# Ordering the last channel groups image by image, moving Toeplitz and piece loads, and whitening 1024 adjacent columns at a time

## The chip, the cores and the metric

The kernel runs on one core of a Trainium2 chip. The metric is the device time of one execution in microseconds. An interval or a share in this document is of that time.

## The reference

The input x has 4 images of 64 channels of 256 x 256 float32 pixels. Two layers follow one another.

```python
# layer 0: a two-dimensional convolution, causal in both directions, one filter per channel
hx = implicit_filter(z, Xw1, Xb1, Xw2, Xb2, Xw3, Xb3, Xwo, Xfreq)   # 256 taps for each channel
hy = implicit_filter(z, Yw1, Yb1, Yw2, Yb2, Yw3, Yb3, Ywo, Yfreq)
k  = outer(hx, hy)                      # separable: a 256 x 256 filter per channel
y  = irfft2(rfft2(x, 512) * rfft2(k, 512) / 512)[:256, :256] + x * bias

# layer 1: whitening of the 64 channels
x1   = y as 64 rows of 4 * 65536 pixels
x1_s = x1[:, ::9]
cov  = x1_s @ x1_s.T / n + 0.01 * I
out  = inverse_sqrt(cov, 5 Newton-Schulz steps) @ (x1 - mean(x1_s))
```

The filter is separable, so the convolution of one channel is a product with one triangular Toeplitz matrix from one side and another from the other side. The whitening needs the samples of every pixel of all images before its first output can be computed.

## The kernel before

**Convolution stage.** The 64 channels are eight groups `g` of eight (`CG`). A step is a group and an image, `(g, n)`; `steps` holds the 32 of them in order. The first six groups run through the four images each; the last two groups are ordered image by image (lines 107 and 108), so that image 0 is complete before image 1 and so on. A step has four channel pairs, `c` = 0, 2, 4, 6. A pair goes through two products. `group` (line 394) computes the first product of one pair and the second product of the pair two places earlier together, in matmuls on halves of the array (line 220), copies the first product out on ScalarE (line 409), and adds x times bias to the second on VectorE (line 412), in place in the x tile. `store` (line 420) then writes the pair to the scratch tensor `y_d[n]` in HBM with two DMAs on SP, and puts nine predicated copies per step in a list `todo`, which take every ninth pixel into `samp[n]`; in the last two groups the list gets 18 of half the size. `pack` works that list off after each group, by the planner's costs: a group earns 2.92 us of credit. `covariance(n)` (line 327) multiplies the samples of an image, 116 matmuls, in the second step of the following image.

**What is loaded when.** All loads of this stage are issued by SP, in program order: the two stores of a group, then an x load, then perhaps a block of Toeplitz matrices, then perhaps a piece. A load of two channels of x has 512 KB. There are four x tiles, and `load_x` runs two steps ahead. Each group's Toeplitz matrices come in eight blocks from the filter taps in HBM (`load_toeplitz`, line 188), into one of three tiles; the table `blocks` says after which group of which step each block is issued.

**Whitening and pieces.** After the last step TensorE does the last second products (`half_group`), packs the last samples with matmuls (`pack_by_pe`), computes the last covariance, and then the chain of small products in `whitening`. `spin` and `busy` are matmuls whose result is not used. What follows is `out = W y + shift`, over 32 pieces of 128 x 4096 elements (2048 KB), eight of each image. The two halves of the partitions are the upper and the lower half of an image. Each of four rounds per piece fills two PSUM banks with four matmuls of 64 x 512; ScalarE evicts one bank and VectorE the other, back into the piece's tile, which is then stored.

**Homes.** A piece lives in one of 13 tiles of 16 KB per partition (`homes`, line 347): tiles of the pools for x (`i`), Toeplitz matrices (`t`), samples (`s`) and a pool `e` whose first tile served as scratch. A tile can take its piece when its old content is used up. `early` (line 378) says after which group of which step SP issues the load of the next piece; nine are in that table and the other four come after the last step. Piece 13 and those after it are loaded by SP into the tile of a piece that has been stored (line 647). The store of the first piece, and those of the pieces that have no successor, are issued by SP; the others by GpSimd (line 644).

Of the kernel before, what the change touches and what calls it, by code (L numbers as in the profile page):

```python
# [38 lines left out]
F32 = mybir.dt.float32  # L39
I32 = mybir.dt.int32  # L40
AF = mybir.ActivationFunctionType
ALU = mybir.AluOpType
# [3 lines left out]
NB, C, L = 4, 64, 256  # L46
P, H2 = 128, 2
EMB, ORDER = 33, 64
PIX = L * L
CG = 8  # L50
# [4 lines left out]
EPS = 0.01  # L55
N_ITER = 5
GW = P + L
FP = 4096

TURN = 6.283185  # L60
# [4 lines left out]
def conv_whiten_kernel(ctx: ExitStack, tc: tile.TileContext, a: dict, out: bass.AP):  # L65
    nc = tc.nc
    x = a["x"]

    const = ctx.enter_context(tc.tile_pool(name="const", bufs=1))
    xpool = ctx.enter_context(tc.tile_pool(name="xpool", bufs=4))  # L70
    epool = ctx.enter_context(tc.tile_pool(name="epool", bufs=2))
    spool = ctx.enter_context(tc.tile_pool(name="spool", bufs=NB))
    tpool = ctx.enter_context(tc.tile_pool(name="tpool", bufs=3))
    o1pool = ctx.enter_context(tc.tile_pool(name="o1pool", bufs=4))
# [3 lines left out]
    y_d = [dram.tile([H2 * C, PIX // H2], F32, tag=f"y{n}", name=f"y_d{n}") for n in range(NB)]  # L78
    g_d = dram.tile([P, GW], F32, tag="g", name="g_d")
    g0_d = dram.tile([2 * CG, GW], F32, tag="g0", name="g0_d")  # L80

# [6 lines left out]
    cols = const.tile([P, 4], F32, tag="cols", name="cols")  # L88
# [9 lines left out]
    bias = const.tile([P, C], F32, tag="bias", name="bias")  # L98

    def load_x(t, g, n, c):  # L100
        nc.sync.dma_start(
            out=t[:, c : c + 2],
            in_=x[n, g][:, c : c + 2],
        )


    steps = [(g, n) for g in range(C // CG - 2) for n in range(NB)]
    steps += [(g, n) for n in range(NB) for g in range(C // CG - 2, C // CG)]

    x_tiles = [xpool.tile([P, CG, H2, L], F32, tag="in", name=f"x{u}") for u in range(4)]  # L110
    for c in range(0, CG, 2):
        load_x(x_tiles[0], *steps[0], c)
        if c == 0:
            nc.sync.dma_start(out=decay, in_=a["decay"])
    nc.sync.dma_start(out=mask, in_=a["mask"])
# [5 lines left out]
    for n in range(NB):  # L121
        t = spool.tile([P, FP], F32, tag="samp", name=f"samp{n}")
        samp.append(
# [9 lines left out]
    def load_pick(lo, hi):  # L133
        for s in range(lo, hi):
            nc.scalar.activation(pick[:, s, :], ident, AF.Copy, scale=rows[:, s : s + 1])

    taps = scratch[:, 11:13, :].rearrange("p a w -> p (a w)")[:, 0:GW]
    nc.gpsimd.memset(taps[:, L:GW], 0.0)  # L140

# [13 lines left out]
    for i in range(3):  # L155
        for u in range(2):
# [3 lines left out]
            arg, k, nxt = (scratch[:, 2 + 3 * i + v, half] for v in range(3))  # L160
# [22 lines left out]
    def new_toeplitz(g):  # L183


        return tpool.tile([P, 2, CG, L], F32, tag="toep", name=f"toep_{g}")

    def load_toeplitz(t, g, f, half, lo=0, hi=CG, issue=nc.sync):
        source, row = (g0_d, f * CG + lo) if g == 0 else (g_d, f * C + g * CG + lo)


        skip = 0 if f == half else HP
        issue.dma_start(
            out=t[half * HP : (half + 1) * HP, f, lo:hi, skip:],
            in_=bass.AP(
                tensor=source.tensor,
                offset=source.offset + row * GW + skip,
                ap=[[1, HP], [GW, hi - lo], [1, L - skip]],
            ),
        )  # L200
# [126 lines left out]
    def covariance(n):  # L327
# [15 lines left out]

    pieces = [(n, q) for n in range(NB) for q in range(PIX // H2 // FP)]


    homes = [
        {"t": (tpool, "toep"), "s": (spool, "samp"), "i": (xpool, "in"), "e": (epool, "extra")}[k]
        for k in "eetssiistitis"
    ]  # L350

    def load_y(i):

        n, q = pieces[i]
        pool, tag = homes[i % len(homes)]
        t = pool.tile([P, FP], F32, tag=tag, name=f"yi_{n}_{q}")
        nc.sync.dma_start(out=t, in_=y_d[n][:, q * FP : (q + 1) * FP])  # L357
        return t

    def load_next():  # L360
        loaded[len(loaded)] = load_y(len(loaded))
# [7 lines left out]


    blocks = {}
    for g in range(1, C // CG):
        first = 16 * g - 14 if g < C // CG - 1 else 16 * g - 22
        for part in range(8):
            k = first + (part * 12 // 8 if g < C // CG - 2 else part)
            blocks[k // 4, k % 4 * 2] = (g, part)

    early = {
        (26, 4): 1, (27, 0): 1, (27, 4): 1, (28, 0): 1, (29, 2): 1, (30, 0): 1, (31, 0): 1, (31, 2): 1, (31, 4): 1
    }  # L380
    orders = [list(range(L // HP)), list(reversed(range(L // HP)))]

# [174 lines left out]
    with tc.manual_schedule(  # L557
        engines={engines.PE, engines.SP, engines.DVE, engines.Activation, engines.Pool}
    ):
        toep = {0: new_toeplitz(0)}  # L560

        for f, lo, hi in ((0, 0, 2), (0, 2, 4), (0, 4, 6), (1, 0, 2), (0, 6, 8), (1, 2, 4), (1, 4, 8)):
            for half in range(2):
                load_toeplitz(toep[0], 0, f, half, lo, hi, nc.scalar if half else nc.sync)
        for c in range(0, CG, 2):
            load_x(x_tiles[1], *steps[1], c)
        for i, (g, n) in enumerate(steps):
            xt = x_tiles[i % 4]
            for c in range(0, CG, 2):
                item = (g, n, c, xt, [])  # L570
                if g == C // CG - 1 and n > 0 and c == 2:
                    covariance(n - 1)
                if len(pending) == 2:
                    group(item, pending.pop(0))
                else:
                    half_group(item, 0)
                pending.append(item)
                if i == 0 and c == 6:

                    fold = const.tile([P, C], F32, tag="fold", name="fold")  # L580
                    nc.vector.tensor_tensor(fold, ident[:, 0:C], ident[:, C:P], ALU.add)

                    nc.scalar.activation(bf[:, 0:1], samp[0][:, 0, 0, C : C + 1], AF.Sqrt)
                if i == 1 and c < CG - 2:
                    load_pick(c // 2 * 3, c // 2 * 3 + 3)

                if i + 2 < len(steps):
                    load_x(x_tiles[(i + 2) % 4], *steps[i + 2], c)
                if (i, c) in blocks:
                    tg, part = blocks[i, c]  # L590
                    if part == 0:
                        toep[tg] = new_toeplitz(tg)
                    lo = part % 2 * CG // 2
                    load_toeplitz(toep[tg], tg, part // 4, part // 2 % 2, lo, lo + CG // 2)
                for _ in range(early.get((i, c), 0)):
                    load_next()
        g, n, c, yt, _ = pending[0]
        for item in pending:
            half_group(item, 1)
            pack(1.0)  # L600
            store(item)

        pack()
        i15 = place(2 * C, rows=C).rearrange("p (u c) -> p u c", u=2)
        for u in range(2):
            nc.gpsimd.tensor_scalar(i15[:, u], ident[0:C, 0:C], 1.5, None, ALU.mult)  # L606
        ones = place(P, rows=C)
        nc.gpsimd.memset(ones, 1.0)
        for lo in range(CG // 2, CG, 2):
            pack_by_pe(g, n, yt, slice(lo, lo + 2))  # L610
        spin(4)
        covariance(NB - 1)
        while len(loaded) < len(homes):
            load_next()
        W, shift = whitening(i15, ones)


    halves = [slice(u * C, (u + 1) * C) for u in range(2)]
    for i, (n, q) in enumerate(pieces):
        yt = loaded.pop(i)  # L620

        v = yt.rearrange("p (v f) -> p v f", v=2)
        o = out[n, q].rearrange("p (v f) -> p v f", v=2)

        part = 512 if i == 0 else 1024 if i == 1 or i > len(pieces) - 3 else 2048
        for w in range(FP // 1024):


            cols = slice(w * 512, (w + 1) * 512)
            po = [  # L630
                psA.tile([P, 512], F32, tag="psA", name=f"po_{n}_{q}_{w}_{u}") for u in range(2)
            ]
            for k in range(2):
                for u in range(2):
                    nc.tensor.matmul(  # L635
                        po[u][halves[k]], lhsT=W[halves[u]], rhs=v[halves[u], k, cols],
                        start=True, stop=True,
                    )
            nc.scalar.activation(v[:, 0, cols], po[0], AF.Identity, bias=shift)  # L639
            nc.vector.tensor_scalar(v[:, 1, cols], po[1], shift, None, ALU.add)  # L640
            end = (w + 1) * 512
            if end % part == 0:

                issue = nc.sync if i == 0 or i + len(homes) >= len(pieces) else nc.gpsimd
                issue.dma_start(out=o[:, :, end - part : end], in_=v[:, :, end - part : end])  # L645
        if i + len(homes) < len(pieces):
            loaded[i + len(homes)] = load_y(i + len(homes))

# [57 lines left out]
```

## Time and profile before

| | |
|---|---|
| median of 3 runs | 902.56 us (902.16 to 902.67) |
| span of the profiled execution | 902.1 us |
| own time of the profiled execution | the profile gives none beside the span |
| TensorE matmuls busy | 781.2 us (87%) |
| VectorE busy | 581.5 us (64%) |
| ScalarE busy | 395.5 us (44%) |
| DMA, whole span | 285.61 MB, 317 GB/s |
| HBM read and written | 149.35 MB and 134.44 MB |
| mean granted TensorE clock | 0.927 |

PE is TensorE's matmul, PEld its weight load, DVE is VectorE, ACT is ScalarE, POOL is GpSimd, SP is SyncE; SPq is SP's sequencer, which issues DMAs. In a list of slices each digit is the busy share of a fortieth of the span in tenths; PEclk is the granted TensorE clock in tenths. In the chain and the timelines a row begins with its start and its length in us. In the table of waits a row ends with the total us, the number and the longest of the waits. In a row by stretches of time the engines come first, and the last three numbers are the granted clock, the busy share of the DMA engines and GB/s.

### The profile page before, as it was taken

The page shows a single profiled execution, that of the slowest core. Times are in us where ns is not written, and L with a number is a line of the kernel's source. Part 1 is how long each engine was busy: PE and PEld are TensorE (multiplying, and loading weights), DVE is VectorE, ACT ScalarE, POOL GpSimd, SP SyncE. Part 2 cuts the span into 40 slices and gives each one's busy share as a digit, 9 for nine tenths or more (in the row PEclk, how much of TensorE's full clock was granted, in tenths as well). Part 3 has the DMA queues.
Part 4 walks back from the last instruction along what each step waited for, and adds up shares of the span by engine and source line. Part 5 has one row for each costly group of instructions (what it writes and reads, how often), then busy time and mean ns, then how long its engine had stood idle before and what let it go on. Part 6 is the DMA issues. An engine that isn't in the chain of part 4 may idle for free.

```text
span 902.1 us, 28046 instructions
## 1 busy us (share of the span) xinstructions
PE 781.2 (87%) x11928; PEld 647.5 (72%) x11928; DVE 581.5 (64%) x801; ACT 395.5 (44%) x676; POOL 14.5 (2%) x40
## 2 busy tenths in 40 slices
PE   8999999999999999999999999999999565666200
PEld 7999999999999999999999999999533111212000
DVE  3487778877888778877888877877688332233200
ACT  2655554545455555545454444442487232233200
POOL 1000000000000000000000000000010000000000
PEclk9999999999999999999999999999999766866755
DMA  7988889798788888888997899979999999999998
GB/s 209 327 262 252 242 261 271 234 273 251 247 263 261 244 264 259 258 250 267 293 275 241 285 351 356 335 237 390 375 401 429 430 432 432 429 434 430 430 430 355
DMA packets 117912, 285.61 MB, mean 317 GB/s; under 512 B 8891, under 2 KB 91116, under 8 KB 110108
## 3 DMA queue, kind: packets, MB, share of 16 engines
q1 hardware_dynamic: 113436, 244.94, 79.0%
q0 software_dynamic: 3056, 37.95, 10.0%
q8 instruction: 95, 1.56, 0.7%
q10 hardware_dynamic: 1296, 0.93, 0.4%
q14 instruction: 29, 0.24, 0.1%
HBM read 149.35 MB, written 134.44 MB: 315 GB/s over the span
## 4 chain that ended last, share of the span: by engine, by line
PE 74%; DMA 11%; another core or an unknown queue 7%; DVE 0%; issue 0%; SPq 0%; ACT 0%; POOLq 0%; DVEq 0%
PE p L220 64%; DMA out_dram<-yi 5%; DMA yi<-y_d 5%; PE po L635 4%; PE pc L333 2%; PE ph L252 1%; PE pk L300 1%; PE spin L442 1%; DMA toep<-g_d 0%; PE busy L152 0%; PE pm L158 0%; SPq L357 0%; DMA scratch<-in_zw_dram 0%; DVE yi L640 0%
## 5 line engine op out<-in xcount | busy, mean ns | idle before, releaser
L220 PE MATMUL p<-toep,x 64*64 64x64 f32 (+3 forms) x5040 | 579.5, 284 | 0.8 <-issue 0.8
L220 PE MATMUL p<-toep,o 64*64 64x64 f32 (+3 forms) x5040 | 579.5, 284 | 0.0
L220 PEld LDWEIGHTS p<-toep,x 64*128 64x128 f32 (+1 forms) x5040 | 535.7, 166 | 24.4 <-issue 1.3
L220 PEld LDWEIGHTS p<-toep,o 64*128 64x128 f32 (+1 forms) x5040 | 536.7, 166 | 10.7 <-issue 0.2
L409 ACT COPY o<-p 64x512 f32<-64x512 f32 x504 | 292.8, 581 | 294.2 <-PE p L220 286.6
L319 DVE COPY_PREDICATED samp<-mask,x 128x464 f32<-128x464 int32 (+3 forms) x351 | 297.2, 847 | 9.8 <-DVE x L412 0.2
L412 DVE SCALAR_TENSOR_TENSOR x<-x,bias,p 128x512 f32<-128x512 f32 x252 | 179.8, 744 | 121.3 <-PE p L220 117.3
L635 PE MATMUL po<-yi,chain 64*64 64x512 f32 x1024 | 143.7, 720 | 60.4 <-DMA yi<-y_d 60.4
L640 DVE TENSOR_SCALAR yi<-po,shift 128x512 f32<-128x512 f32 x128 | 96.1, 751 | 109.0 <-PE po L635 100.7
L635 PEld LDWEIGHTS po<-yi,chain 64*64 64x64 f32 x1024 | 48.0, 162 | 155.2 <-issue 150.5
L639 ACT ACTIVATE yi<-po,shift 128x512 f32<-128x512 f32 x128 | 88.0, 687 | 116.7 <-PE po L635 116.0
L333 PE MATMUL pc<-samp 128*64 128x65 f32 x464 | 14.9, 223 | 0.0
L333 PEld LDWEIGHTS pc<-samp 128*64 128x64 f32 x464 | 14.3, 137 | 0.3
L645 POOL DMA_DIRECT2D out_dram<-yi x19 | 10.5, 554 | 130.5 <-DMA out_dram<-yi 55.1
L606 POOL TENSOR_SCALAR chain<-ident 64x64 f32<-64x64 f32 x2 | 1.0, 519 | 606.6 <-PE ph L252 606.6
L286 DVE COPY o<-ph 64x256 f32<-64x256 f32 x8 | 3.4, 422 | 9.7 <-PE ph L252 9.6
L152 PE MATMUL busy<-idle 128*128 128x128 f32 x64 | 9.4, 307 | 0.0
L152 PEld LDWEIGHTS busy<-idle 128*128 128x128 f32 x64 | 8.9, 222 | 0.2 <-issue 0.2
L300 PE MATMUL pk<-x,pick 128*128 128x56 f32 (+1 forms) x72 | 8.3, 292 | 0.0
L300 PEld LDWEIGHTS pk<-x,pick 128*128 128x128 f32 x72 | 8.1, 192 | 0.1
L442 PE MATMUL spin<-ident 128*128 128x128 f32 x50 | 7.9, 292 | 0.0
L286 ACT COPY o<-ph 64x256 f32<-64x256 f32 x8 | 2.9, 368 | 10.7 <-DMA toep<-g_d 9.2
(93 smaller groups left out, 77.4 us busy)
## 6 DMA issues: line engine op xcount, KB each, us to landing
x<-in_x_dram SPq DMA_DIRECT2D x128, 512.0 KB, 5.3
y_d<-x SPq DMA_DIRECT2D x256, 256.0 KB, 3.5
yi<-y_d SPq DMA_DIRECT2D x32, 2048.0 KB, 15.6
out_dram<-yi POOLq DMA_DIRECT2D x17, 2048.0 KB, 67.7
out_dram<-yi SPq DMA_DIRECT2D x11, 2048.0 KB, 32.9
toep<-g_d SPq DMA_DIRECT2D x28, 256.0 KB, 6.3
toep<-g_d SPq DMA_DIRECT2D x29, 192.0 KB, 5.7
out_dram<-yi SPq DMA_DIRECT2D x4, 1024.0 KB, 32.8
```

The lines of the kernel that those rows point to most:

```text
L152: nc.tensor.matmul(p, lhsT=idle[:, 0:P], rhs=idle[:, P : 2 * P], start=True, stop=True)
L220: mm = nc.tensor.matmul(ps[q : q + w, m, HP * k : L], lhsT=src[parts, k // 2, m * P + q : m * P + q + w], rhs=t[parts, : stop : -1] if k e ...
L300: nc.tensor.matmul(pk[:, b, :, 0:nj], lhsT=pick[:, (s - b) % STEP, :], rhs=yt[:, cs, b, s : s + STEP * (nj - 1) + 1 : STEP], start=(s == 0 ...
L319: nc.vector.copy_predicated(dst, m, src)
L333: nc.tensor.matmul(pc[half], lhsT=samp[n][:, b, j, 0:C], rhs=samp[n][:, b, j, :], start=(b == 0 and j < 2), stop=(b == H2 - 1 and j >= NJ ...
L409: nc.scalar.copy(o1[to], units[u][0][0][fr])
L412: nc.vector.scalar_tensor_tensor(x2[:, c2 + u], x2[:, c2 + u], bias[:, ch : ch + 1], units[u][1][0], ALU.mult, ALU.add,)
L442: nc.tensor.matmul(p, lhsT=ident, rhs=ident, start=True, stop=True)
L635: nc.tensor.matmul(po[u][halves[k]], lhsT=W[halves[u]], rhs=v[halves[u], k, cols], start=True, stop=True,)
L639: nc.scalar.activation(v[:, 0, cols], po[0], AF.Identity, bias=shift)
L640: nc.vector.tensor_scalar(v[:, 1, cols], po[1], shift, None, ALU.add)
L645: issue.dma_start(out=o[:, :, end - part : end], in_=v[:, :, end - part : end])
```

## The change

- `LATE = 3`: the last three channel groups are ordered image by image, before it was two. An image's covariance stays in the second step of the following image, which is now group 6.
- Three x tiles instead of four, and three tiles in the pool `e` instead of two. x is loaded one step ahead instead of two. The tile of a step is `x_of(i)`.
- `blocks` is a table of first places and of the number of groups over which the eight blocks are spread: twelve for the matrices of groups 1 to 6, five for those of group 7. The blocks for the first product still come first.
- `homes` and `early` have a new order: pieces go to `e e e s s s t i t i t i s`, and nine loads are issued from step 23 on, where it was step 26.
- A round of the last stage takes 1024 adjacent columns of a piece instead of 512 columns of either half of it. The output tensor's layout and its rearrangement on the host follow.

```diff
+LATE = 3
-    xpool = ctx.enter_context(tc.tile_pool(name="xpool", bufs=4))
-    epool = ctx.enter_context(tc.tile_pool(name="epool", bufs=2))
+    xpool = ctx.enter_context(tc.tile_pool(name="xpool", bufs=3))
+    epool = ctx.enter_context(tc.tile_pool(name="epool", bufs=3))
...
-    steps = [(g, n) for g in range(C // CG - 2) for n in range(NB)]
-    steps += [(g, n) for n in range(NB) for g in range(C // CG - 2, C // CG)]
+    steps = [(g, n) for g in range(C // CG - LATE) for n in range(NB)]
+    steps += [(g, n) for n in range(NB) for g in range(C // CG - LATE, C // CG)]
...
+    def x_of(i):
+        return x_tiles[(i + 1) % 3]
...
-        for k in "eetssiistitis"
+        for k in "eeessstititis"
...
-    for g in range(1, C // CG):
-        first = 16 * g - 14 if g < C // CG - 1 else 16 * g - 22
-        for part in range(8):
-            k = first + (part * 12 // 8 if g < C // CG - 2 else part)
-            blocks[k // 4, k % 4 * 2] = (g, part)
+    for g, (first, groups) in {
+        1: (2, 12), 2: (18, 12), 3: (34, 12), 4: (46, 12), 5: (57, 12), 6: (69, 12), 7: (82, 5)
+    }.items():
+        for at, part in enumerate((0, 2, 1, 3, 4, 6, 5, 7)):
+            k = first + at * groups // 8
+            blocks.setdefault((k // 4, k % 4 * 2), []).append((g, part))
 
     early = {
-        (26, 4): 1, (27, 0): 1, (27, 4): 1, (28, 0): 1, (29, 2): 1, (30, 0): 1, (31, 0): 1, (31, 2): 1, (31, 4): 1
+        (23, 4): 1, (23, 6): 1, (24, 0): 1, (24, 4): 1, (27, 2): 1, (30, 2): 2, (31, 2): 2
     }
...
-                if g == C // CG - 1 and n > 0 and c == 2:
+                if g == C // CG - 2 and n > 0 and c == 2:
                     covariance(n - 1)
...
-                if i + 2 < len(steps):
-                    load_x(x_tiles[(i + 2) % 4], *steps[i + 2], c)
-                if (i, c) in blocks:
-                    tg, part = blocks[i, c]
+                if 0 < i < len(steps) - 1:
+                    load_x(x_of(i + 1), *steps[i + 1], c)
+                for tg, part in blocks.get((i, c), ()):
...
-        v = yt.rearrange("p (v f) -> p v f", v=2)
-        o = out[n, q].rearrange("p (v f) -> p v f", v=2)
-        part = 512 if i == 0 else 1024 if i == 1 or i > len(pieces) - 3 else 2048
+        v = yt.rearrange("p (w v f) -> p w v f", v=2, f=512)
+        part = 1024 if i == 0 else 2048 if i == 1 or i > len(pieces) - 3 else 4096
...
-                        po[u][halves[k]], lhsT=W[halves[u]], rhs=v[halves[u], k, cols],
+                        po[u][halves[k]], lhsT=W[halves[u]], rhs=v[halves[u], w, k],
...
-            nc.scalar.activation(v[:, 0, cols], po[0], AF.Identity, bias=shift)
-            nc.vector.tensor_scalar(v[:, 1, cols], po[1], shift, None, ALU.add)
-            end = (w + 1) * 512
+            nc.scalar.activation(v[:, w, 0], po[0], AF.Identity, bias=shift)
+            nc.vector.tensor_scalar(v[:, w, 1], po[1], shift, None, ALU.add)
+            end = (w + 1) * 1024
...
-                issue.dma_start(out=o[:, :, end - part : end], in_=v[:, :, end - part : end])
+                issue.dma_start(out=out[n, q][:, end - part : end], in_=yt[:, end - part : end])
```

## The prediction

> **What bounds the kernel now.** I read the page first, in 40 slices of 22.55 us, for who is busy when.
>
> ```profile
> PE   8999999999999999999999999999999565666200
> ...
> PEclk9999999999999999999999999999999766866755
> DMA  7988889798788888888997899979999999999998
> GB/s 209 327 262 252 242 261 271 234 273 251 247 263 261 244 264 259 258 250 267 293 275 241 285 351 356 335 237 390 375 401 429 430 432 432 429 434 430 430 430 355
> ```
>
> There are two stages. For 28 slices TensorE is full and DMA moves about 260 GB/s. For the last ten DMA stands at 430 GB/s and TensorE is half empty. The chain that ended last, in order of time, gives the border:
>
> ```profile
> 83.73 430.31 PE p L220 x7458
> ...
> 599.72 13.88 PE p L220 x240
> 613.60 5.79 PE ph L252 x57
> ...
> 628.52 3.66 PE pc L333 x116
> ...
> 643.25 27.70 PE po L635 x256
> ...
> 672.39 49.18 DMA out_dram<-yi
> ```
>
> The convolution stage is TensorE alone up to 613.6. The L220 pieces of this chain sum to 579.3 us for 126 groups, 4.60 us a group; three covariances of 3.64 us lie between them. Then follow the last half groups, the last covariance and the whitening, and from 643.25 the pieces. The table of waits says what each stage waits for:
>
> ```profile
> PE po L635 <- DMA yi<-y_d: 60.4, 16, 6.3
> ...
> PEld p L220 <- issue: 1.5, 3, 0.8
> ```
>
> L220 waits for no transfer at all. So there are two levers only: the moment at which the whitening ends (TensorE's path), and the rate at which the remaining bytes then move. These are 32 stores and 19 loads of 2.097 MB, 107 MB, or 249 us at 430 GB/s; 647 + 249 = 896, near where the rate falls off (898). Whatever is loaded before 643 is hidden, and 13 homes hold 13 pieces in both kernels. So an earlier start of the piece loads buys nothing by itself. Next, how an x load fares, from the DMA issues in 300 to 480 us and then in 534.8 to 543.5, where piece loads are under way:
>
> ```profile
> x<-in_x_dram SPq DMA_DIRECT2D x40, 512.0 KB, 5.3
> ...
> x<-in_x_dram SPq DMA_DIRECT2D x2, 512.0 KB, 8.9
> ```
>
> The last number is us from issue to landing. Singly these two took 10.0 and 7.9. The timeline of SP shows why: a piece load stands ahead of them in the same queue.
>
> ```profile
> 538.48 0.95 SPq L425 DMA_DIRECT2D y_d<-x  x2
> 539.52 0.49 SPq L101 DMA_DIRECT2D x<-in_x_dram  x1
> 540.12 0.38 SPq L357 DMA_DIRECT2D yi<-y_d  x1
> 542.92 0.88 SPq L425 DMA_DIRECT2D y_d<-x  x2
> ```
>
> Last, rates by stretch (the last two columns are DMA share and GB/s):
>
> ```profile
> 540.00:560.00 20.00, 20.00 (x410) 18.78 (x408) 17.80 (x30) 9.29 (x16) 0.00 (x0) 1.00 1.04 397
> ...
> 645.00:647.00 2.00, 2.00 (x24) 0.72 (x20) 1.75 (x4) 1.54 (x4) 0.00 (x0) 1.00 0.20 77
> 647.00:652.00 5.00, 5.00 (x52) 1.84 (x48) 4.45 (x6) 4.02 (x6) 1.04 (x2) 1.00 1.02 382
> ...
> 656.00:662.00 6.00, 6.00 (x60) 2.14 (x56) 5.25 (x8) 4.80 (x8) 0.53 (x1) 1.00 1.02 335
> ...
> 875.00:885.00 10.00, 0.00 (x0) 0.00 (x0) 0.00 (x0) 0.00 (x0) 0.00 (x0) 0.50 1.02 436
> 890.00:898.00 8.00, 0.00 (x0) 0.00 (x0) 0.00 (x0) 0.00 (x0) 0.00 (x0) 0.50 1.01 416
> ```
>
> At 645 to 647 the loads have drained and the first stores (issued 645.57) have not begun: the handover has no backlog left to remove.
>
> **Prices of the transfers.** At 540 to 560 DMA is full: 7.94 MB in 20 us, 4.35 groups. Each group brings 0.524 MB of x and 0.524 MB of stores, 4.56 MB together; the other 3.38 MB are pieces. A piece at 430 GB/s takes 4.9 us, here I take 5.0; that leaves 12 us for the rest, 2.8 to 3.0 us a group. I take 1.5 for x and 1.5 for the two stores. SP hands over the stores 1.45 us after a group's last matmul, x 2.4 and a piece 2.9 after it; I let a transfer start 2.1 us after its issue. Walked as one queue in order, this gives for x issued at 511.6, 525.0, 531.1, 534.9, 539.5, 549.4 and 557.7 landings of 7.6, 5.8, 4.2, 7.7, 6.1, 7.9 and 4.8; the trace has 8.7, 5.8, 4.3, 10.0, 7.9, 8.1 and 5.0. The walk is short by 0.0 to 2.3, on average 0.8.
>
> **x loaded one step ahead, three buffers.** Before, a channel pair's load is issued eight groups ahead of its group; now four, so that from the issue (2.4 us into the next group) 3 x 4.6 - 2.4 = 11.4 us are left. In the steady stretch it needs 5.3: nothing. SP's order gets no new stall: the third buffer's previous pack operations (L319) are issued one group before SP asks, and ran there from 547.51 to 550.76 behind a group that ended at 546.1, two to three us ahead of the load that now needs them. If VectorE were later than that, SP would hold the load, and the stores queued behind it, one for one.
>
> **Three late groups and the earlier piece loads.** Issues move to (23,4), (23,6), (24,0), (24,4), (27,2), twice (30,2), twice (31,2); (step, channel). Their buffers are free by then (e tiles, samp after each covariance, Toeplitz 5 after (30,2)), so SP does not stop, but every x load behind them does. Walk, from the end of group (23,4) as 0, with ends at 4.6, 9.2, 17.44 (a covariance of 3.64 before it), 22.04, 26.64, 31.24, 35.84, 40.44. Queue: stores 3.55 to 5.05, x 6.55, piece 11.55; 13.05, 14.55, piece 19.55; 21.05, 22.55, piece 27.55; 29.05, x for (25,2) 30.55 (needed 31.24); 32.05, 33.55, piece 38.55; 40.05, x for (25,6) 41.55, needed 40.44: late by 1.1. With the missing 0.8 the two places cost 1.9 together. At (30,2): stores 5.05, x 6.55, pieces 11.55 and 16.55, stores 18.05, x for (31,4) 19.55, needed at 4 x 4.6 = 18.40: late 1.15, with 0.8 more 1.95. Sum 3.9 us on TensorE's path, and so on the whitening and the end. From below: pieces at 436 GB/s (4.8), x at 416 (1.26), stores 1.4, start 1.5: (25,6) has 2.4 us to spare and (31,4) 0.55, so 0. From above, with 2.3 in place of 0.8: 3.4 + 3.5 = 6.9. I take 3.9, the average error.
>
> [...] In the rows TensorE's clock stays 1.00 up to 700 us, through idle pieces of 0.8 us, and falls to 0.72 where TensorE sits idle up to 6.3 us at a time. So I price stalls of 2 us at their length. [...]
>
> **Toeplitz blocks earlier, the last in five groups; covariance one group name earlier; homes.** The 56 loads are the same, behind x on SP. At most two share a group: at 0.22 MB each and 260 GB/s 1.7 us, beside 3.0 in 4.6, so a backlog of 0.1, and x still has 6 us to spare. The buffers of groups 2, 3 and 4 are free when 5, 6 and 7 ask, (14,2), (17,2) and (20,4); the parts for the first product land one step before use. Covariance still follows an image's last pack; nothing. Pack operations: eight steps are halved in both. The x of step 2 is loaded during step 1 instead of step 0: four groups hide it as in every later step; nothing.
>
> **1024 columns at a time.** Matmuls, evictions and the number of stores stay; whole pieces had rows of 16 KB and keep them. Rows double only in the first (2 to 4 KB), second and last two pieces (4 to 8 KB). First: 2.097 MB at 382 against 416 GB/s, 5.49 - 5.04 = 0.45 us. Last two: 4.19 MB, 416 against halfway to 436 (426), 10.08 - 9.85 = 0.2. Second: 656 to 662 moves 335 where 430 was to be had, 0.57 MB or 1.3 us; the second piece's stores and the first new load share it; between 0 and 1.3 I take 0.45, a third. Sum -1.1 (from -0.6 to -2.0). All of it counts, since DMA sets the end.
>
> [...]
>
> **Sum.** 902.1 + 3.9 - 1.1 = 904.9 of span. The profile gives no time for its execution but the span; the median of the runs, 902.56, lies 0.4 above, so 905.3.
>
> **Rivals.**
> *The x loads arrive in time* (not slower). For it: the lower prices leave 0.55 us to spare, and reads and writes may overlap. Against: 10.0 us in the trace where the walk has 7.7. It decides at 11.4 us of landing. Then only rows count: 902.56 - 0.6 to - 2.0, likeliest 901.4; a shorter tail after 898 (229 and 53 GB/s in its last two us) could make it 900.
> [...]
> *The piece loads don't start earlier*: SP waits at (23,4) until image 0's stores have landed. They were issued 5 to 6 us before; the longest such wait was 1.1 us. SP is free again before the next store unless it exceeds 3 us, so the price is near 0, and with the loads later the first stall goes: 905.3 - 1.9 = 903.4.
>
> **Numbers.** About 0.2% (1.8 us) is what a measurement of this kernel can tell from no change. Forecast 0.54 (over 0.2% slower 0.42, within 0.09, faster 0.03); x in time 0.32 (faster 0.21, within 0.11); gate 0.09, slower; loads late 0.05 (slower 0.03, within 0.02). Slower 0.54, within 0.22, faster 0.24. The range goes from 900.0, the low end of the second case, to 909.0: 902.56 + 6.9 - 0.6 = 908.9. The forecast's own range is 903.0 to 908.9.
>
> **What would show it.** Right: L220 waiting for x from in_x, once or twice around 490 and once near 606, 1 to 3 us each; x landings over 11 us there; the pieces' first matmul near 647; 4 KB rows at over 400 GB/s after it. Wrong: no such wait and the first piece at 643; a stall in the steady stretch, which the pack operations would explain; or a store stage off by more than 2 us against 107 MB at its rate, which would mean that rows or homes matter in a way that I did not price.

## The result, and the profile after

The changed kernel takes 909.25 us (median of 5 runs, 905.03 to 909.46) where the kernel before takes 902.61 (902.16 to 902.77): a ratio of 1.0062, 95% interval 1.0046 to 1.0078. It is 6.6 us slower between the medians and 5.6 between the means, which the ratio compares. The profiled execution took 909.27 us with a span of 907.3. In three quarters of the runs the time lies 1.6 to 1.9 us above the span, in the others up to 2.5 and once 3.25. So the profile of before, with its span of 902.1, is probably an execution some 1.3 us slower than the median, whose span would be 902.6 - 1.8 = 900.8.

The page of the kernel after, same slices (here of 22.68 us):

```profile
PE   8999999999999999999999999989999466465300
...
PEclk9999999999999999999999999989999866878755
DMA  7688788788888888889799787698899999999997
GB/s 216 227 274 261 237 269 259 246 251 260 280 265 268 260 271 266 268 265 285 228 396 378 231 283 236 200 398 327 373 403 428 427 436 428 428 433 429 428 433 336
```

DMA is busy near 390 GB/s already in slices 20 and 21, counted from 0 (454 to 499 us), where the first four piece loads now are. TensorE's clock has a dent in slice 26 (590 to 612 us) that before did not have. The chain of waits, in order of time, has two new pieces on TensorE's path:

```profile
457.02 3.64 PE pc L338 x116
460.66 0.49 PE p L225 x18
461.15 2.15 issue
...
592.07 14.23 DMA x<-in_x_dram
606.30 0.14 issue
606.43 12.50 PE p L225 x160
618.94 5.79 PE ph L257 x57
...
648.59 27.70 PE po L638 x256
```

From 643.25 to 648.59 the whitening has moved by 5.3 us, and the span by 5.2. Everything that is lost is lost before the pieces start. The first loss is a stop of 2.15 us in which TensorE waits for nothing that the profile shows, just behind the first covariance. The second is an x load that took 14.2 us. SP's timeline shows that load behind both pieces of (30,2):

```profile
586.16 0.87 SPq L431 DMA_DIRECT2D y_d<-x  x2
587.12 0.44 SPq L102 DMA_DIRECT2D x<-in_x_dram  x1
587.66 0.92 SPq L362 DMA_DIRECT2D yi<-y_d  x2
591.13 0.89 SPq L431 DMA_DIRECT2D y_d<-x  x2
592.07 0.46 SPq L102 DMA_DIRECT2D x<-in_x_dram  x1
```

The third loss is in the stretches around it (TensorE matmul and weight load, then the others; the last three columns are granted clock, DMA share, GB/s; a window that lies across a change of the clock shows a mean):

```profile
598.00:603.00 5.00, 5.00 (x115) 4.55 (x115) 4.24 (x8) 2.32 (x4) 0.00 (x0) 1.00 1.00 371
603.00:606.00 3.00, 0.91 (x9) 0.45 (x5) 2.93 (x6) 2.32 (x4) 0.00 (x0) 0.97 1.04 398
606.00:612.00 6.00, 5.57 (x29) 5.60 (x31) 1.15 (x2) 0.00 (x0) 0.00 (x0) 0.50 1.10 428
612.00:614.00 2.00, 2.00 (x44) 1.88 (x45) 0.00 (x0) 0.00 (x0) 0.00 (x0) 0.83 0.94 401
```

TensorE is idle for 2.9 us, from 603.50 to the next weight load at 606.40, and its clock is at half for 6.83 us, from 605.84 to 612.67. From one group's first weight load to the next, the trace gives: the group with the stop, (24,2), 6.91 us where 4.47 is usual (2.4 lost); the one ahead of the late x, (31,2), 7.58 for 4.45 (3.1 lost); group (31,4) at half clock 7.71 for 4.69 (3.0 lost). Together 8.6 us.

What the two stages wait for, from the table of waits:

```profile
PE po L638 <- DMA yi<-y_d: 64.0, 15, 6.2
...
PE p L225 <- DMA x<-in_x_dram: 2.5, 1, 2.5
...
PE p L225 <- issue: 2.2, 1, 2.2
```

### The profile page after: what moved, and what is told of

Read it like the earlier page. It is cut to its first block, busy times and chain, and to the rows that moved or that the text cites. A ratio compares the mean times of both kernels' runs of the same rounds, so it can differ in the third digit from the quotient of the medians.

```text
span 907.3 us, 28011 instructions
## 1 busy us (share of the span) xinstructions
PE 780.6 (86%) x11928; PEld 648.5 (71%) x11928; DVE 580.6 (64%) x801; ACT 395.1 (44%) x676; POOL 14.2 (2%) x40
## 3 DMA queue, kind: packets, MB, share of 16 engines
q8 instruction: 94, 1.54, 0.7%
## 4 chain that ended last, share of the span: by engine, by line
PE 72%; another core or an unknown queue 11%; DMA 9%; DVE 1%; SPq 1%; issue 1%; ACT 0%; POOLq 0%; DVEq 0%
PE p L225 63%; DMA out_dram<-yi 5%; PE po L638 4%; DMA yi<-y_d 2%; PE pc L338 2%; DMA x<-in_x_dram 2%; PE ph L257 1%; PE pk L305 1%; PE busy L157 1%; PE spin L448 1%; SPq L362 0%; PE pm L163 0%; DMA scratch<-in_zw_dram 0%; DVE yi L643 0%
## 5 line engine op out<-in xcount | busy, mean ns | idle before, releaser
L225 PE MATMUL p<-toep,x 64*64 64x64 f32 (+3 forms) x5040 | 581.4, 285 | 4.7 <-DMA x<-in_x_dram 2.5
L225 PE MATMUL p<-toep,o 64*64 64x64 f32 (+3 forms) x5040 | 581.7, 285 | 0.0
L225 PEld LDWEIGHTS p<-toep,x 64*128 64x128 f32 (+1 forms) x5040 | 537.3, 166 | 28.5 <-DVE samp L324 2.9
L225 PEld LDWEIGHTS p<-toep,o 64*128 64x128 f32 (+1 forms) x5040 | 538.2, 166 | 10.9 <-issue 0.2
L638 PE MATMUL po<-yi,chain 64*64 64x512 f32 x1024 | 140.7, 708 | 64.0 <-DMA yi<-y_d 64.0
```

Of the source, the lines that this page charges most:

```text
L225: mm = nc.tensor.matmul(ps[q : q + w, m, HP * k : L], lhsT=src[parts, k // 2, m * P + q : m * P + q + w], rhs=t[parts, : stop : -1] if k e ...
L638: nc.tensor.matmul(po[u][halves[k]], lhsT=W[halves[u]], rhs=v[halves[u], w, k], start=True, stop=True,)
```

## The experiments

Theory: the losses come from where the piece loads stand, which delays x and TensorE's program in full DMA queues; the clock adds to it. Rival: the order of the steps, the three x tiles or the short lead of x cost something by themselves. Ratios are to the kernel before, run on the same chip; the runs were made on three chips, so that runs are best compared by their ratios, and 0.001 of ratio is 0.9 us. A profile shows one execution of a run.

**The rows alone.** The kernel before with the last stage of the change:

```diff
-        v = yt.rearrange("p (v f) -> p v f", v=2)
-        part = 512 if i == 0 else 1024 if i == 1 or i > len(pieces) - 3 else 2048
+        v = yt.rearrange("p (w v f) -> p w v f", v=2, f=512)
+        part = 1024 if i == 0 else 2048 if i == 1 or i > len(pieces) - 3 else 4096
```

> The kernel before with the last stage alone taken over (1024 adjacent columns a round, rows of 4 KB in the first piece's stores, 8 KB in the second's and the last two's). By the prediction's row term this is 1.1 us faster than before (0.6 to 2.0): about 901.5. By the changed kernel's profile, in which the time from the first piece's matmul to the end fell by only 0.2 us (258.9 to 258.7), it is within 0.3 us of before.

901.48 us against 902.72, ratio 0.9987 (0.9979 to 0.9996): 1.2 us faster, 0.4 to 1.9. The stage itself can be measured over all profiles of this study. From the first piece's weight load to the end of the span it takes 258.97, 259.34 and 259.13 us in the three profiles with the old rows, and 258.40 to 258.89, mean 258.6, in the ten with the new: 0.5 us less. So the rows bring a gain, and 0.5 us of it is seen in their stage; the rest of 1.2 lies within the interval. The traces show where the stage loses part of it again: the first 98.5% of the packets that start in the stage are done 2 us sooner (252.4 us after its start in the rows' own run, 254.3 in before), but the end is set by the last packets, which move at 23 GB/s in the last 4 us of the changed kernel. Why these are so slow is open.

**One of two pieces moved off the last x load.**

```diff
-(30, 2): 2, (31, 2): 2
+(30, 2): 1, (31, 0): 1, (31, 2): 2
```

> The changed kernel with one of the two piece loads of (30,2) moved to (31,0), behind the last x load. Queue theory: x for (31,4) then lands some 5 us sooner, its 3.0 us wait goes and with it the half clock after it (3.0 us), so about 6 us come off: some 903.3; the stop at the first covariance (2.4 us) stays. Rival, that the three x tiles or the order of steps hold x back whatever the pieces do: the wait at (31,4) stays and the time stays near 909.

904.67 us, ratio 1.0028 (1.0015 to 1.0041); span of the profile 901.9. The wait at (31,4) and the half clock are gone in the profile: x for (31,4), now behind one piece, lands 8.2 us after its issue, 3.0 us ahead of its group. Of the time 4.6 us are gone by the medians and 3.1 by the ratios, where 6 were expected; the eight runs go from 902.8 to 908.0. The stop behind the first covariance is still there, 2.2 us in the chain.

**The first four pieces moved behind the covariance.**

```diff
-(23, 4): 1, (23, 6): 1, (24, 0): 1, (24, 4): 1
+(24, 2): 1, (24, 6): 1, (25, 2): 1, (25, 6): 1
```

> The changed kernel with the first four piece loads moved behind the first covariance, two groups apart: (24,2), (24,6), (25,2), (25,6). Theory that TensorE's stop of 2.4 us there is its next 16 KB page of program, late in full DMA queues: the stop goes, about 2.4 us come off, the two later losses stay: some 906.8. Rival, that the covariance itself or the samples it reads are late: the stop stays where it is and the time stays near 909.

906.74 us, ratio 1.0039 (1.0024 to 1.0053): the median is as expected. In the profile the stop is gone. The profiled execution is the fastest of the six, 903.53 us, and it differs from the expectation in one point: x for (31,4) is late as before, 13.5 us after its issue, and TensorE idle for 2.4 us, but the clock stays at 1.00 and group (31,4) takes 4.70 us. The clock in 40 slices has no dent ahead of the pieces, and the table of waits has the wait for x (its longest; the other is at (27,0)):

```profile
PEclk9999999999999999999999999999999876786755
...
PE p L225 <- DMA x<-in_x_dram: 2.4, 2, 2.1
```

So the late x alone does not make the half clock. The list of queues has one called instruction, q8, with 94 packets of 16 KB (1.54 MB) in the trace of the changed kernel, beside 23,856 matmuls and weight loads of TensorE. I take these packets for the pages of TensorE's program, which is the theory of this run; the stop can be set against them. The list of queues for 451 to 460.9 us, first of the changed kernel, which gets no page in that time, then of this run, which does (packets, MB, share):

```profile
q1 hardware_dynamic: 859, 3.18, 93.9%
```

```profile
q1 hardware_dynamic: 1477, 2.20, 71.9%
q8 instruction: 1, 0.02, 0.6%
```

In the traces of the changed kernel, of the run with one piece moved and of the run with x at once (below), the page's packet starts at 460.96, 461.50 and 462.81 us, and each time TensorE stops at the same recorded instruction, the 16064th, with the packet starting one instruction later; it goes on 2.4, 2.4 and 2.9 us after it stopped. Here and in the run with both moves the page starts at instruction 15905 and 15869, 150 to 200 earlier, and nothing stops there. One more figure ties the stop to the page: TensorE goes on 1.4 to 1.5 us after the page's packet has ended, in these three traces, in the two with unused matmuls (below), and in the two profiles with the order of before whose stop is over 0.5 us at that place (before and the run with crowded pieces).

**Something to do for TensorE while x is late.** Unused matmuls on the identity, twenty and then eight:

```diff
+                if (i, c) == (31, 4):
+                    spin(20)        # in the second run spin(8)
```

> The changed kernel with twenty matmuls of 128 x 128 on the identity, whose result is not used, ahead of group (31,4), where TensorE otherwise sits idle for 3.0 us waiting for x. They take about 3.2 us at full clock. Clock theory: x is as late as before, but the clock stays at 1.00 and group (31,4) takes 4.7 us instead of 7.7, so about 3 us come off: some 906.3. Rival, that group (31,4) is slow because its own operands come piecemeal: it still takes 7.7 us, and the time stays near 909 or rises.

908.57 us, ratio 1.0066 (1.0052 to 1.008): no gain. In the profile the clock is 1.00 at this place and group (31,4) takes 4.6 us, but the twenty (each is two matmul instructions in the trace) took 4.73 us, where the wait was 2.9: of the 3.1 us that the clock gave, the surplus took 1.9. The rest is not seen in the time.

> The changed kernel with eight of the unused matmuls ahead of group (31,4) instead of twenty, which took 4.7 us, 2.1 more than the wait for x. Eight take 1.9 us, all of it inside the wait. Clock theory: the clock stays at 1.00 and group (31,4) takes 4.7 us instead of 7.7: about 3 us less than the changed kernel, some 906.3. Rival: the idle 1.1 us that is left still opens the gate, or the group is slow for another reason: near 909.

907.3 us (4 runs from 906.0 to 910.87), ratio 1.0063 (1.0041 to 1.0085). By the ratio, 1.0063 beside 1.0062, the time shows no gain over the changed kernel, though 3 us were expected; the four runs spread by 5 us. The profile of one of them (906.41 us) shows the mechanism: x lands 14.0 us after its issue, as late as ever, the eight take 2.05 us of the wait, and group (31,4) comes at its usual pace, 4.6 us. The same stretch as above, this run:

```profile
603.00:606.00 3.00, 3.00 (x28) 2.58 (x26) 2.93 (x6) 2.32 (x4) 0.00 (x0) 1.00 1.08 408
606.00:612.00 6.00, 5.45 (x115) 5.14 (x113) 2.29 (x4) 0.44 (x1) 0.00 (x0) 1.00 1.09 419
```

115 matmuls from 606 to 612 where there were 29, at clock 1.00 where there was 0.50. Its span is 904.6, 2.7 us less than that of the changed kernel. So the slow group (31,4) is a loss of its own that follows from the idle time and the clock, not from the group's operands: in three profiles x is as late and the group is fast. That filling the wait makes the kernel faster is not shown.

**x handed over ahead of the pieces.** The pieces stay; the four x loads of a step go out together:

```diff
-                if 0 < i < len(steps) - 1:
-                    load_x(x_of(i + 1), *steps[i + 1], c)
+                if 0 < i < len(steps) - 1 and c == 0:
+                    for cc in range(0, CG, 2):
+                        load_x(x_of(i + 1), *steps[i + 1], cc)
```

> The changed kernel, pieces where they are, with the four x loads of the next step issued together after the first group of a step, so that x for (31,4) is handed over ahead of the two pieces of (30,2) and one group earlier. Queue theory: it lands before its group, no wait and no half clock at (31,4): 6 us off, some 903.3, and the stop at the first covariance stays. Rival, that pieces and x share the engines without order: x is still late by 2 us or more and the time stays above 906.

904.9 us, ratio 1.0024 (1.0013 to 1.0034): 3.4 us less than the changed kernel by the ratios, where 6 were expected. No wait for x is left in its profile. The stop behind the covariance stays, and in the profiled execution (906.07 us) it was 2.9 us long and the clock was at half after it, from 465.28 to 468.69:

```profile
462.00:465.00 3.00, 0.56 (x20) 0.42 (x19) 0.23 (x1) 0.00 (x0) 0.00 (x0) 1.00 1.14 453
465.00:469.00 4.00, 3.75 (x40) 3.63 (x41) 0.00 (x0) 0.00 (x0) 0.00 (x0) 0.57 0.96 380
```

**Both moves, and then both with x at once.**

> The changed kernel with both moves: the first four piece loads behind the first covariance, (24,2), (24,6), (25,2), (25,6), and one of the two of (30,2) at (31,0). If the three losses (program page 2.4, x at (31,4) 3.0, half clock 3.0) are all there is, some 8 us come off 909.25, and what is left is the kernel before with the rows' gain: 901 to 902, within 0.5 us of the 901.5 of the rows alone. Rival, that the order of the last three groups, the three x tiles or the Toeplitz times cost something of their own: it stays above 903.

902.96 us, ratio 1.0001 (0.9992 to 1.0010). The expectation named 901 to 902; 1.3 us more than the rows alone are left. In the profile group (26,6) takes 0.9 us longer than usual, since the one behind it, (27,0), waits for its x load, which took 11.3 us to land.

> The changed kernel with the pieces moved as in the run with both moves and also the four x loads of a step issued together. Two moves left 1.3 us over the rows alone, 0.9 us of it seen as a wait at (26,6) whose x load took 10.6 us to land. If that is so, this one comes to the rows alone: 901.5, a ratio of 0.9987. If the order of steps or the three tiles cost something of their own, it stays near 903.

901.69 us, ratio 0.9990 (0.9980 to 1.0000), the same as the rows alone (0.9987). No wait for x is in its table of waits, and L225 has one stop left:

```profile
PE p L225 <- issue: 0.5, 1, 0.5
```

So the order of the three groups, the three tiles, the Toeplitz times and the homes together cost nothing and bring nothing that these runs can tell; the interval leaves room for some 0.9 us either way.

**Pieces crowded before the covariance, in the kernel before.**

```diff
-(26, 4): 1, (27, 0): 1, (27, 4): 1
+(26, 4): 1, (26, 6): 1, (27, 0): 1
```

> The kernel before with the second and third piece loads pulled up by one group, to (26,6) and (27,0), so that three pieces stand in the queue when the first covariance at (27,2) runs; x is loaded two steps ahead there and is not late. Program page theory: the stop at or just behind the covariance grows from 0.7 us to 2 us or more, at the page's arrival; the time rises by 1 to 2 us, to some 904.2. Rival, that the stop in the changed kernel belongs to x's short lead or to the three tiles: nothing stops and the time stays at 902.7.

903.21 us, ratio 1.0001 (0.9992 to 1.0010): the time did not move, against the expectation. The group behind that covariance takes 5.77 us, where the profile of before has 5.17 and 4.45 is usual: the stop is 1.3 us instead of 0.7, less than expected, and in two other profiles with the pieces of before it is 0.2 and 0.3. What orders them is where the page's packet starts: at instruction 18050 and 18060 in those two, 18072 in before and 18090 here, each time ahead of the same instruction, 18113, at which the two longer ones stop. The size does not follow from the number of pieces in the queue alone.

**One step of lead, in the kernel before.**

```diff
-                if i + 2 < len(steps):
-                    load_x(x_tiles[(i + 2) % 4], *steps[i + 2], c)
+                if 0 < i < len(steps) - 1:
+                    load_x(x_tiles[(i + 1) % 4], *steps[i + 1], c)
```

> The kernel before with x loaded one step ahead instead of two, and nothing else (four x tiles, pieces where they were). Its longest x landing was 10.3 us where 11.4 are left: no wait for x, at most 0.5 us of one, and the time stays within 1 us of 902.7. Rival, that the short lead costs by itself, throughout the steady stretch or at each piece: waits for x appear and the time rises by 2 us or more.

903.96 us, ratio 1.0011 (1.0002 to 1.0020): 1.0 us slower, at the edge of what was expected. Its profile has no wait for x, but it is that of the fastest of the ten executions (902.27 us). Where that 1 us lies is open. A short lead alone does not make the 6.6 us.

**A version after the findings.** The rows, and no piece just ahead of the first covariance:

```diff
-(26, 4): 1, (27, 0): 1, (27, 4): 1
+(26, 4): 1, (27, 2): 1, (27, 6): 1
```

> The kernel before with the rows of the change, and its second and third piece loads moved from (27,0) and (27,4) to (27,2) and (27,6), so that none is issued just ahead of the first covariance. Program page theory: the stop of 0.3 to 0.7 us behind that covariance goes: 0.3 to 0.7 us below the rows alone, 901.0, faster than both kernels. Rival: nothing changes, 901.5.

902.38 us, ratio 0.9994 (0.9985 to 1.0003): no gain over the rows alone, where 0.3 to 0.7 us were expected. In its profile stops of up to 0.9 us stand at the second covariance and at three other places instead. The rows alone remain the only version whose interval lies wholly below the kernel before.

## Why the prediction was right or wrong

The forecast was 905.3 us, in a range from 900.0 to 909.0; measured were 909.25. The direction and the first mechanism, x loads held up behind pieces, were right. The size was not: 3.9 us were forecast for waits for x, 3.1 came, and 5.4 us were lost to two things that the sum had at nothing, the stop that I put down to TensorE's program page, and the half clock. That the top of the range comes within 0.25 us of the result is luck, since it was made of 6.9 us of waits for x alone.

- **x at (31,4)** was the right mechanism at the right place. The term was 1.95 us, and 3.1 were lost: the load landed 14.2 us after its issue, where the walk with its correction has 13.4, and 11.2 us were left, where the walk has 11.4. It lies within the term's upper end of 3.5.
- **x at (25,6)**, 1.9 us, did not happen in the changed kernel: the load took 10.8 us and landed 0.85 us before its group. The stop at (24,2) had held TensorE for 2.4 us ahead of it, in which the queue went on; that the wait would have come without the stop is likely, but no run shows it. In the two profiles in which the four pieces stand behind the covariance and x is issued pair by pair, a shorter wait for x stands ahead of (27,0), 0.7 and 0.9 us.
- **The stop that I put down to the program page** is the step that was missing; no term and no rival had it. It measured 2.4 us. A trace of it could be read beforehand: before has a piece of 0.47 us "issue" just behind its first covariance, at 520.7 us, which I took for nothing.
- **The clock** is the step that failed by its condition. I priced stalls of 2 us at their length, from idle pieces of 0.8 us that left the clock at 1.00, and one of 2.9 us came. It cost 3.0 us more, since the clock was at half for 6.83 us. No run shows what the 0.09 for a slower kernel by the clock was priced from; the runs showed in its place that idle times of 2.2 to 2.4 us left the clock at 1.00 in five profiles, and that the two of 2.9 us halved it. The chance was too small: the stall needed to be only 1 us longer than the forecast, and its own bounds reached that.
- **The rows**: 1.1 us forecast, 0.5 in the stage and 1.2 (0.4 to 1.9) in the time. The 4 KB rows of the first piece's stretch ran at 399 GB/s, where I took 416 and before has 382, and I let all of the gain count although the last packets, at 23 GB/s, set the end.
- **The offset** of 0.4 us between span and time was wrong; it is mostly 1.8, and the profile of before was probably a slower execution. The forecast does not depend on it: it is the median of before plus 3.9 less 1.1.
- **Right**: nothing for the order, the buffers, the Toeplitz blocks and the prologue (the first group starts at 21.7 to 22.3 us in the profiles of either order of steps), and no gain from the earlier pieces by themselves.

In sum 8.6 us are lost and 0.5 (rows) gained in the profiled execution. Its convolution stage, from the first group to the last half groups, takes 595.6 us, where that of the kernel before takes 589.8 in its own profile and 587.8 in that of the rows alone: 5.9 to 7.8 more. This is less than 8.6 at least in part because the kernel before has short stops of its own, 1.9 us in its own profile and 0.3 in the other. Less the rows' 0.5 that is 5.4 to 7.3, beside 6.6 between the medians and 5.6 between the means. The runs of the changed kernel spread from 905.0 to 909.5. Different lengths of the stops and of the half clock would do that, but only one of them was profiled.

## What to carry to other kernels

In these runs a bulk load that nobody waited for had a price: x issued behind it in the same queue landed later. An x load, 5.2 us in the median of the changed kernel, took 8.2 us behind one piece and 14.2 behind two. So compare the lead of the small urgent loads with the bulk that can stand in front of them, and hand the urgent ones over first. If the stop of 2.2 to 2.9 us is rightly put down to TensorE's program, count the engine's own program among those who wait when DMA is full. And price a stall of TensorE close to 3 us above its length: the two of 2.9 us here cost 3.0 and 1.6 us more by the clock, where those of 2.2 to 2.4 us left it at 1.00.

## What the runs showed of the hardware that was not expected

- TensorE stopped 2.2 to 2.9 us at one fixed instruction in three traces, in the changed kernel with DMA at 448 GB/s during the stop (461.0 to 463.3 us). There a packet of 16 KB on the queue called instruction starts at 460.96 us and takes 0.88 us, and TensorE goes on 1.46 us after its end. The queue moved 1.54 MB in 94 such packets. In this trace none of the others has a stop over 0.45 us in the convolution stage; this one lies behind the dense covariance (116 matmuls and as many weight loads in 3.64 us) under full DMA. That the packet is TensorE's next stretch of program and the stop its late arrival is my reading of these times; no run shows it directly.
- After idle times of 2.9 us the clock was at half for 6.83 us in the changed kernel and for 3.41 us in the run with x at once. For equal idle time the loss differs. In the traces of the kernel before and of the changed kernel the changes of the clock lie 3.41 us or whole multiples of it apart. In the run with x at once TensorE was at work from the moment the clock fell; in the changed kernel the clock fell 0.56 us before the idle time ended. Why one stretch is twice as long as the other no run here shows.
